# Half-height transposes in the scores' buffers and longer runs of one kind on TensorE, in an attention and mixture-of-experts kernel

## The chip, the cores and the metric

The kernel runs on one core of a Trainium2 chip. The metric is the device time of one execution in microseconds, the median of several runs. The engines are named as in the profile: PE (TensorE's matmuls), PEld (its weight loads), DVE (VectorE), ACT (ScalarE), POOL (GpSimd) and SP (SyncE, which here issues most DMAs).

## The reference

The input is 8 batches of 1024 tokens with 512 features in fp32. A layer norm and an attention with 16 heads of 32 features come first, then a second layer norm and a mixture of 8 experts. Queries, keys and values are not products with weights: they are cosines and sines of scaled features.

```python
theta_q = xh / (1.0 + jnp.abs(w_q)) + b_q + t * phi_q      # same for k
Q = concatenate([cos(theta_q), sin(theta_q)])              # 64 per head; same for K
V = cos_v + sin_v                                          # 32 per head
scores = einsum('bqhd,bkhd->bhqk', Q, K) / scale           # causal
out = einsum('bhqk,bkhd->bqhd', softmax(scores), V)
theta_out = out / (1.0 + jnp.abs(w_out)) + b_out
x = x + cos(theta_out) + sin(theta_out)
# then, on layernorm(x): each token goes to its top 2 of 8 experts, 160 places
# per expert and batch; expert = relu(buf @ W1 + b1) @ W2 + b2, gated, added to x
```

## The kernel before, in words

The attention is worked off in 32 steps `n`, one for each batch `b` and block `c` of 128 features (four heads), `b, c = divmod(n, 4)`. Each step has two head pairs. What follows are the names that matter.

- `scores(pair, h)` makes the transposed scores of one head pair for half `h` of the queries. `tiles_of(h)` gives its tiles: three for half 0, seven for half 1. The last tile of each half is 256 queries wide, the others 512 (one of them is made of 384 and 128). Each tile has two heads. Their keys and queries lie on rows 0 to 63 and 64 to 127, and they are multiplied by two matmuls that use 64 rows and 128 columns of the array each and write one PSUM bank each. The tile's two banks come from the pool `ps_sc`, which has two such tiles. ACT takes the exponential of both into `e`, and DVE zeroes the keys that lie ahead in the tiles on the diagonal (L590, the mask).
- `attend(n, pr, h, es)` multiplies those tiles by the values: two matmuls of 128 rows and 64 columns a tile, one for each head, into one bank of `ps_av`. At its end DVE scales the result into `av_sb`.
- `turn(pr, h, av_sb, p)` transposes `av_sb` by four full 128 x 128 transposes into a bank of the pool `ps_tr` (two banks), and DVE divides by the row sums, which stand among the columns, into `o_p`.
- `qk_pre(n)` transposes the normalized input of a step, again by fours into `ps_tr`, and DVE makes the angles of queries and keys from it (L463, then a shift in L395). `qk_abs`, `qk_sin` and `qk_post` turn them into cosines and sines on ACT and DVE. `v_pre` and `v_post` do the values, `o_pre` and `o_post` the output angle and the sum into `x_mid`, with the statistics of the second layer norm. A step's `qk_pre` runs two steps ahead, its `qk_abs`, `qk_sin` and values one step ahead, and `o_pre` and `o_post` one step behind.
- `router(b)` is a generator that picks the experts of a batch's tokens: `rows` (layer norm on DVE, and a DMA of each row tile to DRAM), `features` (four transposes into `ps_tr` and a copy into `xT`), `parts` (narrow matmuls of 32 columns), `whole` (their sum over the four groups), then the choice on DVE and a prefix sum on PE (`place`). It begins at the end of step `c = 0` of the next batch. Its rows and features fall in the first half of step `c = 1`, the last sums in that step's second half.
- `layernorm1` normalizes a later batch on DVE, in the first halves of steps `c = 0` and `c = 3` (in the first batch, of `c = 1` and `c = 2`).
- `experts` comes last and takes up the span from about 1470 us on. `gather` fetches the tokens of an expert by indirect DMA and transposes them; the first six of these gathers run inside the last attention step.

PE, DVE and ACT run in the order in which the program names their instructions: the kernel sets it by hand. The generators yield between their pieces. `run` takes two pieces of each of its generators in turn, and after each two, one piece of each generator in `aside` (such as the router, `v_pre`, `qk_abs`, `qk_pre`, a layer norm):

```python
e11, av10 = run(scores(pairs[1], 1), attend(n, 1, 0, e10), aside=asides)
```

So scores and products alternate on PE by about two tiles each, with transposes between them.

The exponentials are kept in eight buffers of 512 queries and two of 256 (`ep`), and a head half's product has one of two banks (`ps_av`). [...]

Of the kernel before, what the change touches and what calls it, by code (L numbers as in the profile page):

```python
# [71 lines left out]
def preln_attn_moe_kernel(  # L72
# [61 lines left out]
    avp = to_router.pool("avp", 2, **left)  # L134
# [52 lines left out]
    ps_tr = to_end.pool("ps_tr", 2, space=PSUM)  # L187
# [12 lines left out]
    ps = ps_tr.tile([P, 6 * NCH], F32, name="ps_t")  # L200
# [99 lines left out]
    ps_sc = to_pairs.pool("ps_sc", 2, space=PSUM)  # L300
# [27 lines left out]
    def load_b1():  # L328
        t = own.tile([E * NHC, P], F32, name="vec_in")
        nc.sync.dma_start(t, b1.rearrange("e (c p) -> (e c) p", p=P))  # L330
        ps = ps_tr.tile([P, P], F32, name="ps_t")
        nc.tensor.transpose(ps, t, ident)
        nc.vector.tensor_copy(b1_t, ps)
        two = b1_t.rearrange("p (e h q) -> p e h q", e=E, h=2)
        nc.vector.tensor_tensor(b1_more, two[:, :, 1, :], two[:, :, 0, :], ALU.subtract)
# [3 lines left out]
    def load_mid(b):  # L339

        xt = xmp.tile([P, NTT, D], F32, name="x_mid")
        for h in range(2):
            nc.sync.dma_start(
                xt[:, 4 * h : 4 * h + 4, :], token_tiles(x[b])[:, 4 * h : 4 * h + 4, :]
            )
        st = small.tile([P, NTT, NCH, nc.vector.BN_STATS_DIM], F32, name="st_mid")
        mid_tiles[b] = (xt, st)
# [100 lines left out]
    def qk_pre(n):  # L448

        b, c = divmod(n, NCH)  # L450
        base = bases.pop(n)
        p = qkt.tile([P, 2, S], I32, name="qk_f")
        r = qkt.tile([P, 2, S], I32, name="qk_r")
        for h in range(2):
            yield
            ps = ps_tr.tile([P, 4, P], F32, name="ps_t")
            for t in range(4):
                nc.tensor.transpose(  # L458
                    ps[:, t, :], xn_tiles[b][h][:, t, c * P : (c + 1) * P], ident
                )  # L460
            for i in range(2):
                cols = (slice(None), i, slice(512 * h, 512 * (h + 1)))
                nc.vector.scalar_tensor_tensor(  # L463
                    p[cols], ps.rearrange("p t q -> p (t q)"),
                    inv_qk[:, i * NCH + c : i * NCH + c + 1], base[cols], ALU.mult, ALU.add,
                )
        yield p, r
# [97 lines left out]
    def scores(pair, h):  # L565

        es = []
        for parts in tiles_of(h):
            n = sum(w for _, _, w, _ in parts)
            ps = ps_sc.tile([P, 2, 512], F32, name="ps_s")  # L570
# [21 lines left out]
            yield es  # L592

    def attend(n, pr, h, es):

        vt = v_tiles[n % 2]
        av = ps_av.tile([P, 512], F32, name="av")
        tiles = tiles_of(h)
        for i, parts in enumerate(tiles):
            if i:  # L600
                yield
            for kb, q0, w, at in parts:
                for a in range(2):
                    nc.tensor.matmul(  # L604
                        av[a * 64 : (a + 1) * 64, q0 - 512 * h :],
                        lhsT=vt[:, kb, 2 * pr + a, :], rhs=es[i][:, a, at : at + w],
                        start=kb == 0, stop=i + 1 == len(tiles),
                    )
        av_sb = avp.tile([P, 512], F32, name="av_sb")
        q = 2 * (n % NCH) + pr  # L610
        nc.vector.tensor_scalar(av_sb, av, inv_o[:, q : q + 1], None, ALU.mult)  # L611
        yield av_sb

    def run(*gens, aside=()):


        last, live = [None] * len(gens), list(range(len(gens)))
        while live:
            for i in list(live):
                for _ in range(2):  # L620
                    try:
                        got = next(gens[i])
                        last[i] = got if got is not None else last[i]
                    except StopIteration:
                        live.remove(i)
                        break
                for g in aside:
                    next(g, None)
        return last
# [7 lines left out]
    def turn(pr, h, av_sb, p):  # L637

        ps = ps_tr.tile([P, 4, P], F32, name="ps_t")
        for t in range(4):  # L640
            nc.tensor.transpose(ps[:, t, :], av_sb[:, t * P : (t + 1) * P], ident)  # L641
        av = ps.rearrange("p t (a f) -> p t a f", a=2)
        rec = small.tile([P, 4, 2, 1], F32, name="rec")
        nc.vector.reciprocal(rec, av[:, :, :, DH : DH + 1])
        dst = p.rearrange("p (t a d) -> p t a d", a=HPC, d=DH)
        nc.vector.tensor_tensor(
            dst[:, 4 * h : 4 * h + 4, 2 * pr : 2 * pr + 2, :], av[:, :, :, :DH],
            rec.to_broadcast([P, 4, 2, DH]), ALU.mult,
        )
# [12 lines left out]
    def router(b):  # L662
# [10 lines left out]
        prob = small.tile([P, NTT, E], F32, name="prob")  # L673
# [14 lines left out]
        def features(xn, xT, i):  # L688
            ps = ps_tr.tile([P, NCH, P], F32, name="ps_t")
            for c in range(NCH):  # L690
                nc.tensor.transpose(ps[:, c, :], xn[:, c * P : (c + 1) * P], ident)  # L691
            copy(xT[:, :, i * P : (i + 1) * P], ps)

        def parts(xT):

            ps = ps_tr.tile([P, 2 * P], F32, name="ps_t")
            for c in range(NCH):
                nc.tensor.matmul(  # L698
                    ps[32 * c : 32 * (c + 1), :], lhsT=wr_sb[:, c, :], rhs=xT[:, c, :],
                    start=True, stop=True, tile_position=(0, 32 * c),  # L700
                )
            lg = row2.tile([P, 2 * P], F32, name="lg", bufs=1)
            copy(lg, ps)
            return lg

        def whole(g, lg):

            ps = ps_tr.tile([P, 2, E], F32, name="ps_t")
# [10 lines left out]
        ahead = rows(0)  # L719
        yield "tiles"  # L720
        lg, xT_ = None, None
        for g in range(NTT // 2):
            if g:
                lg = parts(xT_)
            xT_ = row2.tile([P, NCH, 2 * P], F32, name="xT", bufs=1)
            for i in range(2):
                xn = ahead
                if 2 * g + i + 1 < NTT:
                    ahead = rows(2 * g + i + 1)
                features(xn, xT_, i)  # L730
                if i == 0:
                    yield
# [4 lines left out]
        lg = parts(xT_)  # L737
# [50 lines left out]
        place = ps_tr.tile([P, NTT, E], F32, name="ps_t")  # L788
# [119 lines left out]
    def gather(i):  # L908
# [3 lines left out]
        for j in range(2 * nh):  # L912
# [6 lines left out]
            ps = ps_tr.tile([P, NCH, P], F32, name="ps_t")  # L919
            for c in range(NCH):  # L920
                nc.tensor.transpose(ps[:, c, :], xg[:, c * P : (c + 1) * P], ident)  # L921
            nc.vector.tensor_copy(xe[:, :, j // nh, j % nh * P : (j % nh + 1) * P], ps)  # L922
# [153 lines left out]
    def experts(ending):  # L1076
        pools["hp"] = to_end.pool("hp", NHQ, **right)
        pools["ps_p"] = to_end.pool("ps_p", 6, space=PSUM)
# [63 lines left out]
    for n in range(NCK + 1):  # L1142
        live, more, late = n < NCK, n + 1 < NCK, last is not None
# [4 lines left out]
        if live:  # L1148
            pos_n = trig.tile([P, S], F32, name="o_p")
            (e00,) = run(scores(pairs[0], 0))  # L1150
        if n == 0:
            qk_st = rest(qk_pre(1))
            angle(*qk_st)
        if late:
            e11, av10, pos = last
            turn(1, 0, av10, pos)

        if not live:
            break

        if n == 1:
            load_mid(0)


        asides, places, v_box = [], [None], [None]
        if more:
            asides += [keep(places, qk_abs(qk_st)), keep(v_box, v_pre(n + 1))]
        if route is not None and c > 0:
            asides.append(part(route))
        if not more:  # L1170
            asides.append(first_rows)
# [4 lines left out]
        elif c == 3 and b + 2 < B:  # L1176
            asides.append(layernorm1(b + 2, 0))
        av11, e01 = run(
            attend(n - 1, 1, 1, e11) if late else iter(()), scores(pairs[0], 1),
            aside=asides,  # L1180
        )
        for g in asides:
            rest(g)
        if more:
# [12 lines left out]


        (av00,) = run(attend(n, 0, 0, e00))
        if late:  # L1200
            turn(1, 1, av11, pos)
            o_st = o_pre(n - 1, pos)
# [7 lines left out]
        (av01,) = run(attend(n, 0, 1, e01))  # L1210
        turn(0, 0, av00, pos_n)
# [4 lines left out]
        (e10,) = run(scores(pairs[1], 0))  # L1216
        turn(0, 1, av01, pos_n)
# [3 lines left out]

        places = [None]
        asides = [keep(places, qk_pre(n + 2))] if n + 2 < NCK else []
        if route is not None and c > 0:
            asides.append(part(route))
        e11, av10 = run(scores(pairs[1], 1), attend(n, 1, 0, e10), aside=asides)
        for g in asides:
            rest(g)
        if n + 2 < NCK:
            qk_st = places[0]  # L1230
# [6 lines left out]
        last = (e11, av10, pos_n)  # L1237
        pairs = next_pairs if more else None
    turn(1, 0, av10, pos_n)
    (av11,) = run(attend(NCK - 1, 1, 1, e11))  # L1240
    turn(1, 1, av11, pos_n)
# [53 lines left out]
```

## Time and profile before

| | |
|---|---|
| median of 3 runs | 3486.86 us (3486.4 to 3488.84) |
| the profiled execution, its own time | 3486.65 us |
| its span, first to last instruction | 3484.9 us |
| mean granted TensorE clock | 0.992 |
| busy in 100 to 1200 us (attention) | PE 1034.9, DVE 950.4, ACT 806.5, POOL 100.9 us |
| busy in 1500 to 3485 us (experts) | PE 1957.7, DVE 1231.3, ACT 272.1, POOL 228.7 us |
| PE's waits in 100 to 1420 us | for ACT's exponentials 32.6 us; for router rows 15.7, `xT` 12.0, `av_sb` 9.2, `lg` 7.5 us (DVE) |

A row of the costliest groups gives the line, engine and operation, the tile written and the tiles read, the shape, how often, the busy time in us and the mean of one in ns, and the idle time ahead of it with what ended most of it. For a matmul the shape begins with rows x columns of the array that it uses ("64*128"). Each fp32 matmul that is not a transpose appears as two passes, so two records. The ends of matmuls are modelled, so a busy PE may hide short gaps; the distance from one start to the next doesn't.

### The profile page before, as it was taken

The numbers are of one execution on the slowest core, as the hardware profiler recorded it, in microseconds if no ns is written. First come the engines' busy times: TensorE is split into PE (matmuls) and PEld (weight loads), VectorE is DVE, ScalarE is ACT, GpSimd is POOL, SyncE is SP. The second block draws the span as 40 slices with busy tenths as digits, with TensorE's granted clock in tenths as the row PEclk, the third lists the DMA queues.
The fourth block names the chain that finished last, engine by engine and source line by source line (L and its number), as shares of the span: only waits on it lengthen the run. The fifth ranks groups of instructions, "written<-read, shape, count | busy, mean of one in ns | idle before, by whom it ended". The sixth has DMA issues, their size and how long they took to land.

```text
span 3484.9 us, 43387 instructions
## 1 busy us (share of the span) xinstructions
PE 3302.9 (95%) x15974; PEld 2171.9 (62%) x15974; DVE 2469.3 (71%) x5569; ACT 1315.7 (38%) x1609; POOL 391.1 (11%) x346
## 2 busy tenths in 40 slices
PE   3899999999999999889999999999999999999998
PEld 1344444444444444458868868778778688688687
DVE  7897989898989878574684585576566747746844
ACT  5676767676767676420120111111111101101201
POOL 0000202020202020232101101100110111011010
PEclk9999999999999999999999999999999999999999
DMA  4434343434353434142232322422322323322321
GB/s 142 125 93 148 90 154 91 154 91 153 91 178 89 132 87 135 46 137 39 75 106 46 112 61 49 112 55 61 106 46 67 103 43 76 103 38 76 105 40 25
DMA packets 242684, 320.45 MB, mean 92 GB/s; under 512 B 30312, under 2 KB 163112, under 8 KB 230056
## 3 DMA queue, kind: packets, MB, share of 16 engines
q1 hardware_dynamic: 220304, 275.54, 26.7%
q0 software_dynamic: 22080, 42.10, 6.8%
q8 instruction: 127, 2.08, 0.2%
q14 instruction: 85, 0.70, 0.1%
q10 hardware_dynamic: 88, 0.02, 0.0%
HBM read 188.67 MB, written 61.82 MB: 72 GB/s over the span
## 4 chain that ended last, share of the span: by engine, by line
PE 79%; DVE 12%; ACT 5%; issue 2%; DMA 1%; POOL 0%; POOLq 0%; DVEq 0%; ACTq 0%; SPq 0%
PE ps_p L1010 27%; PE ps_p L965 24%; PE av L604 11%; PE ps_s L574 11%; ACT e L580 4%; PE ps_t L641 2%; DVE e L590 1%; PE ps_t L921 1%; PE ps_t L458 1%; PE ps_t L691 1%; DVE qk_c L405 1%; DVE av_sb L611 1%; DVE qk_r L405 1%; DVE xn L679 0%; PE ps_t L698 0%
## 5 line engine op out<-in xcount | busy, mean ns | idle before, releaser
L580 ACT ACTIVATE e<-ps_s 128x1024 f32<-128x1024 f32 (+1 forms) x640 | 564.5, 937 | 389.8 <-PE ps_s L574 385.9
L574 PE MATMUL ps_s<-qk 64*128 64x512 f32 (+3 forms) x3072 | 607.7, 512 | 62.0 <-ACT e L580 40.4
L1010 PE MATMUL ps_p<-w,hid 128*128 128x256 f32 x2560 | 569.4, 380 | 0.0
L604 PE MATMUL av<-e,v 128*64 128x512 f32 (+3 forms) x3072 | 557.4, 499 | 5.8 <-DVE e L590 5.8
L1010 PEld LDWEIGHTS ps_p<-w,hid 128*128 128x128 f32 x2560 | 484.5, 190 | 66.3
L574 PEld LDWEIGHTS ps_s<-qk 64*128 64x128 f32 x3072 | 277.9, 187 | 326.1 <-issue 160.2
L1010 PE MATMUL ps_p<-w_t,hid 128*128 128x256 f32 x1920 | 430.5, 379 | 1.3 <-DVE w_t L886 1.3
L604 PEld LDWEIGHTS av<-e,v 128*64 128x64 f32 x3072 | 195.5, 138 | 322.1 <-issue 264.2
L1010 PEld LDWEIGHTS ps_p<-w_t,hid 128*128 128x128 f32 x1920 | 361.7, 190 | 49.7 <-DVE w_t L886 2.1
L965 PE MATMUL ps_p<-xe_s,t 128*128 128x256 f32 (+1 forms) x1024 | 299.8, 436 | 3.4 <-DVE t L950 3.4
L965 PE MATMUL ps_p<-xe,w 128*128 128x256 f32 (+1 forms) x1024 | 298.3, 434 | 0.2
L965 PE MATMUL ps_p<-xe,t 128*128 128x256 f32 (+1 forms) x1024 | 296.8, 433 | 0.0
L657 POOL DMA_INDIRECT slot_d<-token,slot x128 | 149.4, 1167 | 1146.9 <-issue 636.9
L590 DVE TENSOR_TENSOR e<-e,seen 128x256 f32<-128x256 f32 (+1 forms) x384 | 184.4, 510 | 118.3 <-ACT e L580 115.1
L965 PEld LDWEIGHTS ps_p<-xe_s,t 128*128 128x128 f32 x1024 | 194.6, 191 | 87.3 <-DVE t L950 7.9
L1039 ACT COPY p<-ps_p 128x256 f32<-128x256 f32 x40 | 14.7, 368 | 612.5 <-PE ps_p L1010 612.5
L965 PEld LDWEIGHTS ps_p<-xe,t 128*128 128x128 f32 x1024 | 194.4, 190 | 80.5
L965 PEld LDWEIGHTS ps_p<-xe,w 128*128 128x128 f32 x1024 | 192.8, 190 | 82.5 <-DVE hid L983 5.9
L1032 POOL DMA_INDIRECT out_dram<-y,slots x80 | 126.4, 1580 | 671.5 <-DVE y L1027 528.6
L914 POOL DMA_INDIRECT xg<-xn_d,source x80 | 78.3, 979 | 1026.8 <-PE ps_t L921 1017.1
L922 DVE COPY xe<-ps_t 128x512 f32<-128x512 f32 x80 | 55.3, 691 | 194.9 <-PE ps_t L921 194.3
L980 ACT ACTIVATE p<-ps_p,b_t 128x256 f32<-128x256 f32 (+1 forms) x128 | 65.5, 512 | 330.5 <-DVE y L1026 170.0
(193 smaller groups left out, 3874.0 us busy)
## 6 DMA issues: line engine op xcount, KB each, us to landing
w<-in_L_ffn_W_dram SPq DMA_DIRECT2D x256, 256.0 KB, 3.2
qk<-qk_c SPq DMA_DIRECT2D x128, 256.0 KB, 4.5
qk<-qk_r SPq DMA_DIRECT2D x128, 256.0 KB, 4.6
w<-in_L_ffn_W_dram SPq DMA_DIRECT2D x64, 512.0 KB, 7.1
qk_base<-base_d SPq DMA_DIRECT2D x29, 1024.0 KB, 5.1
xn_d<-xn SPq DMA_DIRECT2D x72, 256.0 KB, 2.0
x_mid<-in_L_attn_x_dram SPq DMA_DIRECT2D x16, 1024.0 KB, 8.5
out_dram<-x_mid SPq DMA_DIRECT2D x8, 2048.0 KB, 11.7
```

The source lines that it names most:

```text
L405: nc.vector.scalar_tensor_tensor(out, f.bitcast(F32), LIFT, s, ALU.add, ALU.mult)
L574: nc.tensor.matmul(ps[:, a, at : at + w], lhsT=pair[r, 1, kb * P : (kb + 1) * P], rhs=pair[r, 0, q0 : q0 + w], start=True, stop=True,)
L580: nc.scalar.activation(e, ps[:, :, :n], AF.Exp, scale=UNIT * UNIT / math.sqrt(2 * DH))
L590: nc.vector.tensor_tensor(own_keys, own_keys, k, ALU.mult)
L604: nc.tensor.matmul(av[a * 64 : (a + 1) * 64, q0 - 512 * h :], lhsT=vt[:, kb, 2 * pr + a, :], rhs=es[i][:, a, at : at + w], start=kb == 0, ...
L641: nc.tensor.transpose(ps[:, t, :], av_sb[:, t * P : (t + 1) * P], ident)
L657: nc.gpsimd.indirect_dma_start(out=slot_d[b], out_offset=bass.IndirectOffsetOnAxis(ap=idx, axis=0), in_=src, in_offset=None,)
L914: nc.gpsimd.indirect_dma_start(out=xg, out_offset=None, in_=xn2_d[i % 2], in_offset=bass.IndirectOffsetOnAxis(ap=source[:, e, j0 + j, None ...
L965: nc.tensor.matmul(ps, lhsT=weights[:, k, :], rhs=rows[:, k, :], start=k == 0, stop=k == 1)
L980: nc.scalar.activation(p1, product(b11, a11), AF.Identity, bias=b1_t[:, e * NHC + q : e * NHC + q + 1])
L1010: nc.tensor.matmul(ps, lhsT=hs[k][:, part, cols], rhs=ws[k][weight], start=k == 0, stop=k == NHQ - 1,)
L1032: nc.gpsimd.indirect_dma_start(out=out, out_offset=bass.IndirectOffsetOnAxis(ap=meta[:, e, jj[r], 0:1], axis=0), in_=ys[r], in_offset=None ...
```

## The change

The transposes of the attention stage are cut in halves of 64 rows: the upper 64 rows of a block go to one bank and the lower 64 to the other, by two transposes that use 64 rows and 128 columns of the array, as a score matmul does. Their target is a tile of `ps_sc`, which now has three tiles; `ps_tr` is opened only for the experts. The router's sums take tiles of `ps_sc` too. `turn` takes both query halves of a head pair at once, and `qk_pre` both token halves. The order is written out in longer runs: three product tiles, five score tiles, three products, four scores, three products, one score, a `turn`, the eight remaining products, five scores, a `turn`, three products, five scores, and then `qk_pre` in one piece at the step's end. Asides now go on by one piece after each score tile. `rows` are made two at a time. The pools `avp` and `once` change to fit (three `av_sb`, single buffers for `st_mid` and `prob`).

```diff
-    ps_tr = to_end.pool("ps_tr", 2, space=PSUM)
+    ps_sc = to_pairs.pool("ps_sc", 3, space=PSUM)
+    def two_banks():
+        return ps_sc.tile([P, 2, 512], F32, name="ps_s")
+    def by_halves(turned, src):
+        for a in range(2):
+            r = slice(a * 64, (a + 1) * 64)
+            nc.tensor.transpose(turned[:, a, :], src[r, :], ident[r, r])
...
 def qk_pre(n):
-        for h in range(2):
-            yield
-            ps = ps_tr.tile([P, 4, P], F32, name="ps_t")
-            for t in range(4):
-                nc.tensor.transpose(
-                    ps[:, t, :], xn_tiles[b][h][:, t, c * P : (c + 1) * P], ident
...
+        ps = two_banks()
+        for t in range(NTT):
+            by_halves(
+                ps[:, :, t * 64 : (t + 1) * 64],
+                xn_tiles[b][t // 4][:, t % 4, c * P : (c + 1) * P],
+            )
...
-    def turn(pr, h, av_sb, p):
-        ps = ps_tr.tile([P, 4, P], F32, name="ps_t")
-        for t in range(4):
-            nc.tensor.transpose(ps[:, t, :], av_sb[:, t * P : (t + 1) * P], ident)
+    def turn(pr, halves, p):
+        ps = two_banks()
+        for t in range(NTT):
+            by_halves(
+                ps[:, :, t * 64 : (t + 1) * 64],
+                halves[t // 4][:, t % 4 * P : (t % 4 + 1) * P],
+            )
...
+        products = [attend(n, 0, h, es[h], halves[0]) for h in range(2)]
+        if late:
+            products.insert(0, attend(n - 1, 1, 1, e11, halves1))
+        ahead = [scores(pairs[0], h, es[h]) for h in range(2)]
...
+        def with_asides(count):
+            for _ in range(count):
+                some(1, *ahead)
+                for g in asides:
+                    next(g, None)
+        if late:
+            some(3, *products)
...
+            with_asides(5)
+        some(2, absolutes)
+        if late:
+            some(3, *products)
+        with_asides(4)
+        some(2, absolutes)
+        some(3, *products)
+        with_asides(1)
...
+        if late:
+            turn(1, halves1, pos)
+            o_st = o_pre(n - 1, pos)
...
+        some(NTT + 2, *products)
...
+        with_asides(5)
+        turn(0, halves[0], pos_n)
...
+        some(3, attend(n, 1, 0, es[0], halves1))
+        with_asides(5)
+        if n + 2 < NCK:
+            qk_st = rest(qk_pre(n + 2))
```

Here `some(k, *gens)` takes the next `k` pieces of the generators, one generator after the other. The router's `features` handles two row tiles in one piece:

```diff
-        ahead = rows(0)
+        ahead = [rows(0), rows(1)]
         yield "tiles"
...
+                ps = two_banks()
+                for i, xn in enumerate(xns):
+                    for c in range(NCH):
+                        at = (NCH * i + c) * 64
+                        by_halves(ps[:, :, at : at + 64], xn[:, c * P : (c + 1) * P])
+                for a in range(2):
+                    copy(
...
+            if g + 1 < NTT // 2:
+                ahead = [rows(2 * g + 2), rows(2 * g + 3)]
             if g:
                 whole(g - 1, lg)
             yield
```

The last batch's router and all gathers but the first expert's keep full transposes.

## The prediction

> **What bounds the kernel now.** I read the page's busy shares first, then its costliest groups, then the busy times by stretch, then the timelines of three engines inside one step.
>
> ```profile
> PE 3302.9 (95%) x15974; PEld 2171.9 (62%) x15974; DVE 2469.3 (71%) x5569; ACT 1315.7 (38%) x1609; POOL 391.1 (11%) x346
> ...
> L574 PE MATMUL ps_s<-qk 64*128 64x512 f32 (+3 forms) x3072 | 607.7, 512 | 62.0 <-ACT e L580 40.4
> ```
>
> TensorE is busy 95% of the span, but the experts (from 1470 us on) are not touched; only the attention stage before them counts. There one batch is four steps. I cut it at the four starts of the wide sine of L482 (the third is batch 3's second; columns: span of the stretch, then busy us of PE, PEld, DVE, ACT, POOL):
>
> ```profile
> 555.17:594.78 39.60, 38.53 (x218) 17.15 (x218) 35.80 (x76) 31.81 (x32) 14.30 (x12) 1.00 0.32 80
> 594.78:645.10 50.32, 45.30 (x280) 21.91 (x278) 42.59 (x95) 31.92 (x32) 0.20 (x2) 1.00 0.53 154
> 645.10:687.87 42.76, 39.97 (x233) 17.92 (x230) 33.86 (x75) 31.95 (x33) 0.00 (x0) 1.00 0.53 165
> 687.87:728.70 40.84, 39.75 (x226) 18.15 (x228) 37.46 (x86) 31.81 (x32) 5.01 (x4) 1.00 0.30 79
> ```
>
> I call them A, B, C, D: 173.5 us a batch. PE is the fullest, but DVE is at 80 to 92% and ACT at 63 to 80%, both in program order: whoever speeds up PE soon waits for them. Now the inside of PE's busy time (start, us, then the group):
>
> ```profile
> 604.45 1.99 PE L574 MATMUL ps_s<-qk 64*128 64x512 f32 x8
> 606.37 1.94 PE L604 MATMUL av<-e,v 128*64 128x512 f32 x12
> 608.25 0.66 PE L458 MATMUL ps_t<-ident,xn 128*128 128x128 f32 x4
> 608.83 1.99 PE L574 MATMUL ps_s<-qk 64*128 64x512 f32 x8
> 610.75 0.66 PE L458 MATMUL ps_t<-ident,xn 128*128 128x128 f32 x4
> 611.34 0.65 PE L604 MATMUL av<-e,v 128*64 128x256 f32 x4
> ```
>
> Three shapes of the array alternate: 64*128 (scores), 128*64 (products), 128*128 (transposes).
>
> [...] inside a run, pairs of 512-column passes start 0.429 us apart, so eight score records (four pairs) are 1.72 us of work, but the next group starts 1.92 us later (604.45 to 606.37): 0.20 us a run of scores. Products: the run at 606.37 is also 1.72 us of work and takes 1.87, 0.156 a run. Four transposes start 0.109 apart, 0.44 us, and take 0.585, 0.148 a run. [...] two 64-row, 128-column score passes, each with its own load, start every 0.109 us. [...]
>
> **The change, part by part.**
> *Fewer mode changes.* In the order of instructions up to the experts' first product, runs of one mode go from 254 scores, 252 products, 260 full-array and 28 narrow router runs to 223, 159, 37 and 28: half transposes use the scores' mode and stand next to scores. Cost before 254 x 0.20 + 252 x 0.156 + 260 x 0.148 + 28 x 0.14 = 132.5 us; after 223 x 0.20 + 159 x 0.156 + 37 x 0.148 + 3.9 = 78.8. **Minus 53.7 us**, all on PE's path.
> *Half transposes.* Two per former one. A pair loads 128 columns in each row group and streams 64. Not shown before: at best 0.055 us a pair (half the columns), at worst 0.218 (no overlap). I take 0.109, the pair of score passes: no change.
> *VectorE.* Same elements: two reciprocals (0.198) and two fixed parts fewer a step, under 0.6 us; the 512-element operations of L463 and L692 stay four and two in number at 0.74 and 0.68. The strided 64-blocks I take at the same price (range 0 to +10%, 0.5 us a step). DMA queues and POOL keep their instructions. The router's rows now store in twos (256 KB each, 2.0 us to landing on the page); with two buffers the next two wait for both stores, which land 2 us before DVE gets there. SP's loads of qk are issued 10 us and more ahead of use, and `load_mid(0)`, issued later by half a step, is used a step later.
> *ScalarE.* The same instructions; their distance decides what PE waits for. From the timeline of ACT:
>
> ```profile
> 592.33 1.14 ACT L399 ACTIVATE v_p<-v_p,split_c 128x1024 f32<-128x1024 uint16 x1
> 593.49 1.28 ACT L482 ACT_TABLE_LOAD   x1
> 594.78 2.00 ACT L482 ACTIVATE qk_c<-qk_c,quarter_c 128x2048 f32<-128x2048 f32 x1
> 596.69 1.89 ACT L402 ACTIVATE qk_r<-qk_r 128x2048 f32<-128x2048 int32 x1
> 598.49 1.99 ACT L402 ACTIVATE t_r<-t_r 128x1024 f32<-128x1024 int32 x2
> 600.49 1.28 ACT L580 ACT_TABLE_LOAD   x1
> 602.16 2.43 ACT L580 ACTIVATE e<-ps_s 128x1024 f32<-128x1024 f32 x3 [0.38 <-PE ps_s L574]
> ```
>
> From 592.33 to 602.16 no exponential runs: 9.8 us. I laid one new step out by hand: PE at 0.86 us a wide score tile (0.43 a narrow one) plus the run costs; exponentials every 0.92 us (0.50), the first 0.27 after its scores' last pass is issued, its buffer free 1.08 after its start. Zero is the first run of products.
> - P3 to 2.7; five score tiles to 6.8, unhindered: the third buffer removes the stall of 0.56 that three tiles have before. P3 to 9.6, four tiles to 13.2, P3, one tile, turn at 16.0 to 16.9, eight products to 23.1.
> - ACT runs without a pause from 10.8: four exponentials, two squares, the narrow exponential, square, table, sines, table, and starts the next exponential at 26.9. PE has three free buffers for the next run, filled at 25.4; the fourth tile waits until 27.9: **2.5 us**. Before, this stretch loses 0.56 + 1.66.
> - The rest is PE's: the next step begins at 38.1. Work 33.2, ten runs 1.8, waits 2.8 and seams.
>
> So a plain step is 38.1. VectorE in the same step: `qk_pre`, now one block at the step's end, is through L463 and L395 4.6 us after PE has gone on; it is in time for the next step's masks (4.9). Then the kinds of stretches:
> - A: 38.1, and in six of seven batches 1.3 of lateness that D's layernorm leaves. 39.3 (39.6 before).
> - D: `places` takes a buffer among five score tiles and its readers follow `v_post` on DVE: +1.3. 39.4 (40.8).
> - C: `parts` and `whole` do the same at the end of the router: +1.9, exp of `prob` +0.3. 40.3 (42.8).
> - B: the router's tiles. DVE's chain ahead of them:
>
> ```profile
> 611.21 2.70 DVE L463 SCALAR_TENSOR_TENSOR qk_f<-ps_t,inv_qk,qk_base 128x512 int32<-128x512 f32 x4
> ...
> 616.07 1.22 DVE L395 TENSOR_SCALAR qk_r<-qk_f 128x2048 int32<-128x2048 int32 x1
> 617.21 1.11 DVE L669 BATCH_NORM_AGGREGATE mv<-st_mid 128x2 f32<-128x24 f32 x8
> ...
> 621.25 0.55 DVE L679 TENSOR_SCALAR xn<-x_mid,mv,rstd 128x512 f32<-128x512 f32 x1
> ```
>
> The aggregates, the roots and the first row of tokens (5.2 us from 616.07's end) now follow that late block: 4.6 + 1.1 + 2.9 + 0.5 = 9.1 us into the step, when PE has been at the first `features` since 3.7: 5.4 us of wait, against 1.2 at 621.85 before. What follows in the ring of three (score, `parts`, `features`, score, `whole`) costs PE 1.0 at the first `parts` (its xT copies stand behind a mask and `v_pre`), 1.6 at the second `features` (rows behind a mask and a bias addition), 0.8 at the fifth score tile, then little. Work of features, parts and sums 5.1, their mode changes 2.1. Step c = 1 reaches its sine 16.0 later than a plain one: **54.1 (50.3)**.
>
> Sum: A to D 173.1 against 173.5 a batch, seven times: -3. The first batch has no router; its stretches of 42.9 and 39.8 fall to about 39.0 and 38.3: -5. The start and the last step (six gathers, whose PE waits of 5.15, 3.32 and 1.27 us depend on landings) I take as unchanged, plus or minus 5. Experts: same instructions, 0. Together -8 of the profiled execution's 3486.65 (span 3484.9; the median, 3486.86, lies within 0.3): **3478**. So of 53.7 us saved on modes, about 45 come back as waits.
>
> **Rivals.** A measurement here tells 0.2%, 7 us, from nothing.
> 1. *Slower: VectorE's round trip in every lap of the router.* Transposes and router sums now draw on the scores' three buffers, so a late DVE copy stops scores too. If laps three and four each wait 2.6 us as the first pair does (1.0 + 1.6), with none of them caught up, B gains 5.2 more, times seven, 36: 3514. It decides once DVE is still over 2 us behind PE at the third `parts`. For it: 42.6 us busy in B. Against: P3 between laps two and three gives DVE 2.7 us.
> 2. *Faster: the mode changes come through whole.* If ACT's trigonometry is covered (a shorter backlog at the narrow tile) and the router waits no longer than now, all 53.7 stay: 3433. For it: half of the runs of products end. Against: 9.8 us without exponentials against 9.3 us of work and buffers.
> 3. *Halves do not overlap.* 1016 pairs at +0.109 are 111 us; the third of them ahead of the eight products hides in ACT's wait: +78, 3556. Against: the 0.109 of score passes. At 0.055 a pair it turns into some -28 instead.
> That the order doesn't change is excluded: the counts of runs come from it.
>
> **How the numbers follow.** Forecast 0.42 (3455 to 3497), rival 1 0.28, rival 2 0.22, rival 3 0.08. Half of the forecast's mass lies below 3480, a quarter within 7 us of 3487. Faster 0.22 + 0.22, and a little of rival 3's other end: 0.45; same 0.13; slower 0.42. The range 3430 to 3535 leaves out the lower half of rival 2's spread and rival 3. The likeliest case alone: 3455 to 3497.
>
> **What would show it.** Runs of products in a plain step take work + 0.156 five times, not eight; half transposes 0.87 us per eight tiles; fourth score tile of the second head pair waits about 2.5 us for L592's exponential; the first `features` of a batch waits about 5 us for a row of L684; stretches of some 38 to 40, 54, 40, 39. It is wrong if B is under 51, if A is under 37 or over 41, or if half transposes start over 0.12 apart.

## The result, and the profile after

The changed kernel takes 3544.16 us (median of four runs, 3540.82 to 3551.25) against 3486.76: ratio 1.0166, interval 1.0148 to 1.0184, some 57 us slower. The forecast was 3478. The profiled execution took 3551.25 us with a span of 3549.5 and a mean granted clock of 0.957; before it had 3486.65, 3484.9 and 0.992.

The page of the kernel after, first the busy shares, then the granted clock by fortieths of the span, then the group of the scores:

```profile
PE 3276.8 (92%) x16986; PEld 2175.1 (61%) x16986; DVE 2462.8 (69%) x5439; ACT 1308.0 (37%) x1609; POOL 389.7 (11%) x346
...
PEclk9899989898989898899999999999999999999999
...
L586 PE MATMUL ps_s<-qk 64*128 64x512 f32 (+3 forms) x3072 | 615.2, 535 | 47.5 <-ACT e L592 23.3
```

PE is busy 26 us less than before although it has more instructions, and it waits more: 92% of a longer span. Its clock row, a row of 9s before, has an 8 in many slices of the attention, and the same 3072 score passes take 535 ns each instead of 512. The four stretches of batch 3 (columns as in the prediction; the last three are granted clock, DMA share, GB/s):

```profile
568.09:609.44 41.35, 38.01 (x248) 17.56 (x248) 36.87 (x74) 31.33 (x33) 12.46 (x13) 0.91 0.32 77
609.44:671.34 61.90, 53.02 (x362) 24.88 (x360) 44.45 (x92) 31.99 (x33) 0.00 (x0) 0.82 0.50 154
671.34:714.01 42.67, 39.12 (x256) 18.62 (x254) 33.61 (x72) 31.80 (x34) 0.00 (x0) 0.92 0.43 124
714.01:752.14 38.13, 33.05 (x224) 15.42 (x220) 34.30 (x78) 31.44 (x33) 4.68 (x4) 0.99 0.33 84
```

All four had a clock of 1.00 before. Only D keeps it, and D is the one that became clearly shorter (40.8 to 38.1). Means over seven batches (six for D), in us:

| stretch | before | forecast | after | after minus forecast | times | in all |
|---|---|---|---|---|---|---|
| A | 39.6 | 39.3 | 40.6 | +1.3 | 7 | +9 |
| B | 50.7 | 54.1 | 60.2 | +6.1 | 7 | +43 |
| C | 43.1 | 40.3 | 42.6 | +2.3 | 7 | +16 |
| D | 40.8 | 39.4 | 38.1 | -1.3 | 6 | -8 |

With the first batch (forecast -5, measured +6.7 with the start) and the end from the last wide sine on (forecast 0, measured +4.1) this makes the 73 us between forecast and profiled execution, but for 3 us by which the forecast's one batch lay below the mean.

What PE waited for, over the whole span (in all, times, longest):

```profile
PE ps_s L200 <- DVE xn L684: 64.3, 15, 6.0
PE ps_s L200 <- DVE av_sb L622: 52.7, 17, 8.9
PE ps_s L737 <- DVE lg L730: 24.8, 7, 3.5
```

In batch 3 these are waits of 2.6 to 6 us: 3.8 at the seam of D and A, 2.6 at the seam of A and B, 6.0 and 2.9 in B, 3.5 in C. The timeline of PE in B shows what follows one (start, us, the group, the idle time before it):

```profile
606.01 0.41 PE L200 MATMUL ps_s<-ident,av_sb 64*128 64x64 f32 x8
609.00 0.69 PE L200 MATMUL ps_s<-ident,av_sb 64*128 64x64 f32 x8 [2.58 <-DVE av_sb L622]
609.62 8.98 PE L614 MATMUL av<-e,v 128*64 128x256 f32 x36
618.53 4.32 PE L586 MATMUL ps_s<-qk 64*128 64x512 f32 x24
...
629.72 0.71 PE L200 MATMUL ps_s<-ident,xn 64*128 64x64 f32 x16
630.36 2.80 PE L614 MATMUL av<-e,v 128*64 128x512 f32 x12
633.09 1.13 PE L586 MATMUL ps_s<-qk 64*128 64x512 f32 x4
640.18 1.12 PE L200 MATMUL ps_s<-ident,xn 64*128 64x64 f32 x16 [5.97 <-DVE xn L684]
643.90 1.08 PE L725 MATMUL ps_s<-xT,wr_sb 128*32 128x256 f32 x8
647.89 1.22 PE L200 MATMUL ps_s<-ident,xn 64*128 64x64 f32 x16 [2.91 <-DVE xn L684]
```

The eight products after the turn take 8.98 us where the same 36 records take 6.2 in a stretch at full clock (shown below). The 16 half transposes take 0.71 ahead of the wait for the rows and 1.12 after it. The record of the clock says why: the granted share is 0.5 from 608.36 to 615.18 and from 639.08 to 656.14, and 1.00 between them. The wait from 606.4 to 609.0, at the seam of A and B, cost 2.6 us by itself and then 2.7 in the eight products.

I counted such half-clock spells in the clock record from 100 us to the experts' first product, and PE's busy time in them. Before: 4 spells, 20.5 us long, PE busy for 19.7 of them. After: 36 spells, 252.6 us, **PE busy for 197.3 us of them**. In them a pair of 512-column product passes starts 0.853 us after the last, outside them 0.429 (medians). So at full clock that work would take about half as long, and the spells cost PE some 99 us by this estimate. (The expectation of e1 says 34 spells and 86 us: it counts up to 1470 us and with another estimate of the work.)

The record also shows when the clock falls. Its 84 changes between the first and the last lie on one grid of 3.413 us, to within 2 ns. Of the grid's intervals between 100 and 1440 us, PE entered 322 at full clock. In 33 of them it was busy for 47% of the interval or less, and half clock followed every one. In the other 289 it was busy for 48% or more, and half clock followed none. In other runs the border is less sharp: in the kernel before the clock falls after intervals of up to 56% and stays after some from 41% on, in e6 it falls after up to 62% and stays after some from 48% on; the ends of matmuls are modelled. So in the changed kernel the place of a wait in the grid counted too: it sets how much of each interval is left (see D's wait of 1.84 us, below).

### The profile page after: what moved, and what is told of

Read it like the earlier page. It is cut to its first block, busy times and chain, and to the rows that moved or that the text cites. A ratio compares the mean times of both kernels' runs of the same rounds, so it can differ in the third digit from the quotient of the medians.

```text
span 3549.5 us, 45378 instructions
## 1 busy us (share of the span) xinstructions
PE 3276.8 (92%) x16986; PEld 2175.1 (61%) x16986; DVE 2462.8 (69%) x5439; ACT 1308.0 (37%) x1609; POOL 389.7 (11%) x346
## 4 chain that ended last, share of the span: by engine, by line
PE 68%; DVE 16%; ACT 9%; DMA 4%; issue 3%; POOL 0%; SPq 0%; DVEq 0%; POOLq 0%; ACTq 0%
PE ps_p L1043 26%; PE ps_p L998 24%; PE av L614 7%; PE ps_s L586 7%; ACT e L592 4%; DVE qk_f L476 2%; DVE e L602 2%; DMA xn_d<-xn 1%; PE ps_s L200 1%; DMA slot_d<-token,slot 1%; DVE st L367 1%; DVE qk_r L407 1%; PE ps_t L954 1%; ACT qk_c L495 1%; ACT qk_f L411 1%
## 5 line engine op out<-in xcount | busy, mean ns | idle before, releaser
L586 PE MATMUL ps_s<-qk 64*128 64x512 f32 (+3 forms) x3072 | 615.2, 535 | 47.5 <-ACT e L592 23.3
L614 PE MATMUL av<-e,v 128*64 128x512 f32 (+3 forms) x3072 | 565.8, 516 | 6.7 <-DVE e L602 6.7
L614 PEld LDWEIGHTS av<-e,v 128*64 128x64 f32 x3072 | 211.5, 144 | 318.4 <-issue 278.0
L1017 ACT ACTIVATE hid<-hid 128x256 f32<-128x256 f32 (+1 forms) x128 | 60.1, 470 | 317.4 <-DVE hid L1016 317.4
```

The lines of the kernel that those rows point to most:

```text
L586: nc.tensor.matmul(ps[:, a, at : at + w], lhsT=pair[r, 1, kb * P : (kb + 1) * P], rhs=pair[r, 0, q0 : q0 + w], start=True, stop=True,)
L614: nc.tensor.matmul(av[a * 64 : (a + 1) * 64, q0 - 512 * h :], lhsT=vt[:, kb, 2 * pr + a, :], rhs=es[i][:, a, at : at + w], start=kb == 0, ...
L1017: nc.scalar.activation(h11, h11, AF.Relu)
```

## The experiments

The theory: **the waits halve PE's clock**, and that is what the forecast lacks. The rivals: the waits themselves are too long because rows come late (rival 1's round trip), or because DVE's layer norm of a later batch delays `av_sb`; and the half transposes cost more than they save. Times of before in the same sessions were 3488 us.

**e1_warm: keep PE busy in its longest waits.** Nothing is moved. PE gets more to do: pairs of spare matmuls into the tile that the transposes or sums then overwrite.

```diff
+    def keep_warm(ps, count):
+        for _ in range(count):
+            for a in range(2):
+                r = slice(a * 64, (a + 1) * 64)
+                nc.tensor.matmul(
+                    ps[:, a, :], lhsT=ident[r, :], rhs=inv_v[r, :], start=True, stop=True
+                )
...
+                keep_warm(ps, (5, 2, 0, 0)[g])        # features
+                keep_warm(ps, 3 if g == 3 else 0)     # whole
-            turn(1, halves1, pos)
+            turn(1, halves1, pos, 3 if c in (0, 3) else 0)
```

> Spare score-shaped matmuls (64 rows, 128 columns of the array, 512 wide) are put into the tile that the next transposes or sums overwrite: five pairs ahead of the first features of a batch, two ahead of the second, three ahead of the last whole, three ahead of turn(1) in the steps with a layer norm. No result uses them. Theory 1, the slow clock: the waits for VectorE are about those of my sum, and the rest of the loss (some 66 us over the forecast) is PE running at half clock after each of them, 86 us of work done in 34 slow spells; with PE kept busy the clock stays up and the time falls by 40 to 60 us, to about 3495, B to some 55, A to 39. Theory 2, the waits alone: the spells lie in stretches where PE would have waited for VectorE anyhow; then the time moves by less than 10 us, about 3540.

Measured: 3500.13 us, ratio 1.0033 (1.0021 to 1.0046): **44 us less than the changed kernel, with more work on PE**. Its stretches A and B (batch 3):

```profile
557.05:595.72 38.67, 38.02 (x262) 17.92 (x264) 36.31 (x74) 31.32 (x32) 14.36 (x11) 1.00 0.32 83
595.72:651.14 55.42, 50.85 (x384) 23.84 (x384) 43.90 (x92) 31.99 (x33) 2.90 (x2) 1.00 0.56 172
```

The clock is 1.00 again. Over all batches A to D are 38.5, 55.9, 41.5, 38.9: close to the forecast's 39.3, 54.1, 40.3, 39.4. PE's timeline at the place shown above:

```profile
592.29 2.74 PE L206 MATMUL ps_s<-inv_v,ident 64*128 64x512 f32 x12
594.87 0.78 PE L200 MATMUL ps_s<-ident,av_sb 64*128 64x64 f32 x16
595.58 6.24 PE L622 MATMUL av<-e,v 128*64 128x256 f32 x36
```

The spare matmuls fill the wait for `av_sb`, and the 36 product records behind it take 6.24 us instead of 8.98. Half-clock spells fall from 36 to 14, PE's busy time in them from 197.3 to 58.0 us. Half of the difference is 70 us, of which 44 show in the time. The theory holds. What remains in B, 55.9, is time at nearly full clock (0.91 to 1.00 in its seven batches).

**e2_router_late: start the router's tiles five score tiles later in step c = 1**, then two pieces at a time, so that the rows are made before PE asks.

```diff
-        if route is not None and c > 0:
+        if route is not None and c == 1:
+            asides += [later(10, part(route))] * 2
+        elif route is not None and c > 0:
             asides.append(part(route))
```

(`later(k, gen)` yields `k` times before it goes on to `gen`. It stands in the list twice, so ten yields are five score tiles.)

> In step c = 1 the router's pieces begin five score tiles later, at the sixth, and go on two at a time, so that VectorE has caught up with its block at the step boundary when PE reaches the first features. Both theories: the wait of about 6 us for the first rows goes, and with it most of the half-clock spell. B falls from about 60 to 51 to 53, the whole by 50 to 65 us, to about 3485. If instead the rival of the round trip in every lap rules (scores stopped by late copies through the shared three tiles), B stays above 57 and the gain is under 20 us.

Measured: 3511.23, ratio 1.0072 (1.0055 to 1.0088), 33 us less than the changed kernel. B fell to 53.8, not to the 51 to 53 expected, and the saving is below the 50 to 65 expected. The row waits went, and a new one came, in PE's timeline:

```profile
634.73 0.64 PE L725 MATMUL ps_s<-xT,wr_sb 128*32 128x256 f32 x8 [3.46 <-DVE xT L710]
```

The first `parts` now waits 3.5 us for its `xT` copy, and 29 spells remained, with PE busy for 170.8 us in them. Removing one wait did not restore the clock here, with another of 3.5 us in its place and those of A and C untouched.

**e3_norm_moved and e4_late_and_moved: move the later batch's layer norm out of the first halves of steps c = 0 and c = 3** into the second halves of c = 1 and c = 3, to free DVE ahead of `av_sb` and rows; e4 has e2's edit too. In the first batch the layer norm of step 0 is left out, since step 2 makes it again.

```diff
-        elif c == 0 and b + 1 < B:
-            asides.append(layernorm1(b + 1, 1))
-        elif c == 3 and b + 2 < B:
-            asides.append(layernorm1(b + 2, 0))
...
+        if b > 0 and c == 1 and b + 1 < B:
+            asides.append(layernorm1(b + 1, 1))
+        elif c == 3 and b + 2 < B:
+            asides.append(layernorm1(b + 2, 0))
```

> layernorm1 of a later batch goes from the first halves of steps c = 0 and c = 3 to the second halves of c = 1 and c = 3. Theory: the waits of turn(1) for av_sb (52.7 us in all) come from the layer norm that stands ahead of av_sb in VectorE's queue, and each is followed by a slow spell over the eight products. A falls from 41.4 to about 38.5; C rises by up to 2 since its sums wait longer behind the norm; the whole falls by 5 to 30 us, to about 3525. Rival: VectorE is the bound there anyway, and the wait only moves to another place: within 10 us of 3544.

> The edits of e2 and e3 together. If VectorE's order is the cause and the mode savings of 54 us are real, the time falls below that of before: B about 51, A about 38.5, C about 42, D 38, 170 a batch against 173.5, so about 3460 to 3475. If the savings in mode changes were not real or are bound up with the waits, it stays at 3487 or above.

Both expectations failed. e3 took 3575.09, ratio 1.0244 (1.0227 to 1.0261), 31 us slower than the changed kernel; e4 3536.36, ratio 1.0135 (1.0118 to 1.0151), 25 slower than e2 alone. PE's waits in e3:

```profile
PE ps_s L586 <- ACT e L592: 52.0, 31, 3.1
PE ps_s L586 <- DVE qk_f L476: 19.2, 13, 2.8
PE ps_s L200 <- DVE av_sb L622: 17.0, 11, 8.9
```

The wait that it was made for did shrink, from 52.7 to 17.0 us. But ACT's exponentials now hold PE up for 52.0 us (23.3 in the changed kernel), and `qk_f` for 19.2 (2.9); there are 42 half-clock spells. The second halves end with `qk_pre`. That the layer norm delayed DVE there, and that the exponentials came late because their masks and angles did, is argued, not traced further.

**e5_full_height: the order of the changed kernel with full transposes**, in `turn` and `qk_pre`.

```diff
-            by_halves(
-                ps[:, :, t * 64 : (t + 1) * 64],
-                halves[t // 4][:, t % 4 * P : (t % 4 + 1) * P],
-            )
+            nc.tensor.transpose(
+                ps[:, t // 4, t % 4 * P : (t % 4 + 1) * P],
+                halves[t // 4][:, t % 4 * P : (t % 4 + 1) * P], ident,
+            )
```

> The changed kernel with full 128 x 128 transposes again in turn and qk_pre, into the same two-bank tiles and in the new order; the router keeps its halves. Theory: the half height is worth its price in the sum: each of 96 groups of eight transposes would take 0.87 us plus one more change of mode (0.15) instead of 0.49, about 0.53 us, 51 us in all, of which the 32 groups ahead of the eight products may hide in ACT's wait: 3575 to 3595. Rival: what is saved on PE comes back as waiting wherever it is, because VectorE sets the pace: within 10 us of 3544.

Measured: 3563.91, ratio 1.0214 (1.0197 to 1.0231), 20 us slower than the changed kernel. A `turn` in its timeline of PE:

```profile
589.52 1.09 PE L643 MATMUL ps_s<-ident,av_sb 128*128 128x128 f32 x8
```

Eight full transposes take 1.09 us, the 16 halves 0.71: the halves are cheaper, and so no cause of the loss. The difference is below the 31 to 51 us expected and above the rival's 10; that part of these groups lies ahead of a wait for ACT or DVE would explain it, but is not shown.

**e6_late_warm: e2's later start, and e1's filling** in the waits that then remain (three pairs at the turn in c = 0 and 3, four at the first `parts` of a batch, three at the last `whole`).

> The router begins late as in e2, and spare matmuls stand ahead of the turn in the steps with a layer norm (three pairs), ahead of the first parts of a batch (four) and ahead of its last whole (three). Slow-clock theory: e2's gain of 33 and e1's of 44 are for different places in part (e1's of A and C remain to be had), so about 3475 to 3490, B to 51, C to 41, A to 39. Rival, the waits alone: no better than e2, 3505 to 3515.

Measured: 3475.09, ratio 0.9959 (0.9945 to 0.9973), 69 us below the changed kernel and below the one before. Stretches 38.4, 51.8, 41.0, 39.2; 13 spells, with PE busy for 65.6 us in them. As expected.

**e7_sums_late: e6 with the router's last sums five score tiles later**, unfilled, to take away the `lg` wait rather than fill it.

```diff
-            asides.append(part(route))
+            asides.append(later(5, part(route)))
```

> As e6, and the router's last sums and its places come five score tiles later in the second halves of steps 1 and 2 (behind turn(0), where VectorE no longer has the trigonometric products and v_post in front of them); no spare matmuls at the last whole. C loses its wait of 3.5 us for lg and falls to about 39.5, the rest as e6: 3460 to 3480, which would be below the kernel before (3487). If VectorE is the pace-setter everywhere, C stays over 41 and the time with e6's.

Measured: 3484.9, ratio 0.999 (0.9981 to 0.9999): 10 us worse than e6, and C at 41.5 instead of 39.5, so the expectation failed. Its waits of PE:

```profile
PE ps_s L594 <- ACT e L600: 33.6, 17, 2.2
PE ps_s L756 <- DVE lg L744: 17.5, 16, 2.0
```

The longest `lg` wait shrank from the 3.5 us of the changed kernel to 2.0, and the half-clock spells stay few without filling there (15, in e6 13). But the sums now stand among the last score tiles of the step; the waits for `lg` in all rose from 7.3 in e6 to 17.5, and those for ACT from 18.6 to 33.6.

**e8_full_height_warm: e6 with e5's full transposes.** With the clock restored, this prices the halves in a kernel with few half-clock spells.

> e6 with the full 128 x 128 transposes in turn and qk_pre, the edit of e5: the price of the half height where the clock is kept up. Theory: in e5 slow spells and VectorE's waits blurred it (20 us of the 51 worked out); here PE sets the pace in more places, so 25 to 45 us over e6's 3475, about 3500 to 3520, D up by about 1.5 to 2.2. Rival, VectorE and ScalarE set the pace: again 20 us or less.

Measured: 3493.41 (15 runs, 3486 to 3506), ratio 1.0017 (1.0009 to 1.0025), 18 us above e6. The rival's figure, 20 us or less, held. In the profiled executions, which are 27 us apart, A, B, C and D are 1.1, 1.5, 0.9 and 0.8 us longer. So the halves of `turn` and `qk_pre`, with the changes of mode that full transposes bring back, are worth about 0.5% of the time in both pairs of kernels, with many half-clock spells (e5) and with few (e8).

**e9_first_batch: e6 without the layer norm that step 0 makes ahead of time.** In the first batch the second half of batch 1 is normalized in step 0 and again in step 2 (in the kernel before as well). The edit leaves out the first, as e3 did; filling at the turn is added in steps 1 and 2.

```diff
-        elif c == 0 and b + 1 < B:
+        elif c == 0 and 0 < b < B - 1:
             asides.append(layernorm1(b + 1, 1))
...
-            turn(1, halves1, pos, 3 if c in (0, 3) else 0)
+            turn(1, halves1, pos, 3 if c in (0, 3) or n < 3 else 0)
```

> e6 without the layer norm of step 0, which is made again in step 2, and with spare matmuls ahead of turn(1) in steps 1 and 2 too. The 8.9 us in which that turn waits for av_sb in step 1 come from VectorE's backlog of the first steps: 4 to 12 us under e6, about 3465. If the backlog has another cause (the angles of the first block), no change from 3475.

Measured: **3463.23 (3461.32 to 3464.18), ratio 0.9926 (0.9913 to 0.9939)**, the fastest of all, 81 us below the changed kernel and 25 below the one before. Its A and B of batch 3:

```profile
547.30:586.08 38.78, 38.01 (x262) 17.86 (x264) 36.44 (x74) 31.31 (x32) 15.09 (x10) 1.00 0.32 82
586.08:637.71 51.63, 49.24 (x372) 23.36 (x372) 43.83 (x92) 31.76 (x33) 3.77 (x3) 0.97 0.60 185
```

The mean stretches are 38.5, 51.3, 41.0 and 39.2; A is where it was in e1 and B 8.9 below the changed kernel's, 0.7 above the one before. But the wait for `av_sb` that the edit was made for is still there. PE's waits at that turn, in e3 (no layer norm in step 0, no filling) and in e9 (2.7 us of spare matmuls ahead of it):

```profile
128.74 0.69 PE L200 MATMUL ps_s<-ident,av_sb 64*128 64x64 f32 x8 [8.91 <-DVE av_sb L622]
129.32 0.69 PE L200 MATMUL ps_s<-ident,av_sb 64*128 64x64 f32 x8 [6.33 <-DVE av_sb L630]
```

So the layer norm of step 0 does not cause it: DVE works without a pause ahead of this `av_sb`, on the base of the next angles and on the layer norm of step 1 itself among others; which of them counts was not tested. The first four steps take 171.0 us, in e6 175.3. The layer norm left out shortens the first of the four by about 2 us, in e3 as in e9; the fourth is 3 us shorter than in e6, where the filling in step 2 lets 36 product records take 6.24 us instead of 8.90 (single profiles). Of the other 8 us below e6, about 5 lie behind the last wide sine and 3 in B, neither of which the edit touches; they stay open (e6's own runs spread from 3468.6 to 3479.7).

All kernels with their half-clock spells from 100 us to the experts' first product:

| kernel | us | half-clock spells | their length, us | PE busy in them, us |
|---|---|---|---|---|
| before | 3486.76 | 4 | 20.5 | 19.7 |
| after | 3544.16 | 36 | 252.6 | 197.3 |
| e1 | 3500.13 | 14 | 71.7 | 58.0 |
| e2 | 3511.23 | 29 | 194.6 | 170.8 |
| e3 | 3575.09 | 42 | 249.2 | 198.0 |
| e4 | 3536.36 | 36 | 208.2 | 188.2 |
| e5 | 3563.91 | 36 | 218.5 | 177.3 |
| e6 | 3475.09 | 13 | 78.5 | 65.6 |
| e7 | 3484.9 | 15 | 81.9 | 70.7 |
| e8 | 3493.41 | 12 | 78.5 | 65.2 |
| e9 | 3463.23 | 10 | 47.8 | 39.8 |

## Why the prediction was wrong, step by step

**The failed step: the sum takes PE's speed as constant.** Every term of work was at the durations of a kernel whose attention ran at full clock, and the change was to open waits of 5.4, 2.5 and 1.6 us by the prediction's own account. The sum has no term for what PE does after them. The clock record of the changed kernel has it: spells at a granted 0.5, of 3.4, 6.8, 10.2, 17.1 and 20.5 us, multiples of 3.41 on one grid; those up to 1440 us began after intervals in which PE was busy for 47% or less. In the wait of 2.6 us at the seam of A and B, the clock fell when PE had stood for 1.9 us. e1 puts the price at 44 us, of the 66 that the median missed the forecast by.

D shows a wait that brings a spell in some places and none in others. There PE waits 1.84 us for ACT in every batch. In the changed kernel the grid cuts all six of these waits so that PE is busy for 52% or more of both intervals, and no spell follows; in e6 and e9, one of 3.4 us follows in four of six, and D takes 39.7 to 39.8 instead of 38.1. Where the grid cuts the wait there is not shown. The same place in the changed kernel and in e6:

```profile
722.10 0.70 PE L586 MATMUL ps_s<-qk 64*128 64x256 f32 x4 [1.84 <-ACT e L592]
723.01 1.99 PE L586 MATMUL ps_s<-qk 64*128 64x512 f32 x8 [0.21 <-ACT e L592]
...
350.18 0.70 PE L594 MATMUL ps_s<-qk 64*128 64x256 f32 x4 [1.85 <-ACT e L600]
351.10 3.60 PE L594 MATMUL ps_s<-qk 64*128 64x512 f32 x8 [0.21 <-ACT e L600]
```

**The waits.** Those of the router were foreseen in place and cause; the others only in part:
- The first `features` waits 5.97 us for a row of L684 (forecast 5.4).
- The wait of 2.5 for ACT at the fourth score tile was laid out for every plain step. In D it comes at the third, where `places` has a buffer too: 1.84 us, and 0.21 at the next (lines above). In A and B it does not come, nor does it in e1's A and B at full clock. There PE waits for `av_sb` just before, which may be what lets ACT catch up.
- The second `features` waits 2.91 (1.6). The prediction let the row stores land 2 us before DVE gets there. They do not: DVE's timeline has the row itself held up.

```profile
639.49 1.00 DVE L684 TENSOR_SCALAR xn<-x_mid,mv,rstd 128x512 f32<-128x512 f32 x2
647.20 1.17 DVE L684 TENSOR_SCALAR xn<-x_mid,mv,rstd 128x512 f32<-128x512 f32 x2 [1.16 <-DMA xn_d<-xn]
```

  This 1.16 is nearly the size of the miss. More row buffers might take it away; that was not tried.
- Missed: the turns at the two seams of A wait 3.8 and 2.6 us for `av_sb`, behind the layer norm on DVE (e3, which moves it, cuts these waits from 52.7 to 17.0 in all). The prediction had 1.3 us of lateness there. It also had 1.9 for `parts` and `whole` in C together, where `whole` alone waits 3.5 for `lg`.

In these waits the engines took nothing that the program names behind. PE stood 5.97 us for the first rows and took the score tile behind them at 641.06, after the 16 transposes of 640.18. ACT was in its table loads and sines from 712.71 to 721.02 while the score tile begun at 717.47 stood. DVE stood 1.16 us ahead of the row at 647.20, and copied the `lg` that PE had ended at 644.98 behind it, at 649.22.

Of B's 6.1, e1 returns 4.3. The other 1.8 is the size of the longer waits at the two `features` (0.6 and 1.3), but the missing wait for ACT and the shorter transposes work the other way in B, so this split is not shown. A and C: e1 gives back 2.1 of A's and 1.1 of C's; C's other 1.2 goes with the longer wait for `lg`.

**The mode changes** (from one shape of the array to another) were right. In the changed kernel, at full clock, the record behind a 512-column score pass starts 0.423 us after it if its shape is the same (a half transpose or a narrower score pass), and 0.519 if it is a product (medians). A run of 16 product records is 2.575 us of work and takes 2.73, a run of 20 score records 3.44 and takes 3.64: 0.155 and 0.20 as before. So the price of a run did not change and, by the count of runs, the 53.7 us were saved on PE. No run measures them by themselves: with full transposes e8 is level with the kernel before (1.0017), so what e6 and e9 gain can't be put down to the modes alone. D takes 38.1, the figure laid out by hand for a plain step, but that is luck. The forecast for D was 39.4, and D is made of other terms: 2.05 of waits for ACT, and 3.0 of the wait for `av_sb` that begins in D (in batch 3 from 749.1 to D's end at 752.14).

**The half transposes** were mis-sized: at full clock a pair starts 0.062 us after the last (the median in the changed kernel), near the lower bound of 0.055 and not at 0.109, which a full transpose of the same block takes. A group of 16 halves takes 0.64 us to the next run (629.72 to 630.36). In the half-clock spells a pair takes 0.107. By the prediction's count, 1016 pairs at 0.047 less are 48 us of PE's time. In the whole time, e5 and e8 show 20 and 18 us for three quarters of the pairs and the changes of mode together. The error was in the kernel's favour: it hid a part of the loss.

**The first batch** was to give 5 us and cost 6.7. PE waits 8.9 us there for `av_sb`; the prediction carried the gain of a plain step into a batch whose own waits it had not laid out. The layer norm of step 0 is not their cause (e3 and e9 above). **The end**, +4.1, lies inside the 5 allowed.

**Rivals.** Rival 1 had the sign, slower, by 27, but not the mechanism: laps three and four were not to catch up because DVE would be behind. In the trace they run without a wait (the third `parts` starts at 661.37, at full clock), and it is DVE that waits for PE, 2.88 us at 654.96; the half clock (639.08 to 656.14) lies on the first two laps. Filling the waits, which leaves DVE's work as it is, takes 4.3 us out of B. Rival 2's size, 3433, was not reached by any kernel here, e9 at 3463 being the nearest. Rival 3 is excluded by the 0.062; its aside, some -28 at 0.055 a pair, has the right sign. Of the forecast's own signs of being wrong, B under 51 and A under 37 or over 41, the second did not show in the mean A of 40.6 but does in five of the seven batches (41.4 to 41.8). For B there was no upper bound, and the loss came there. One reading in the prediction is off without effect: the 5.2 us of aggregates and roots run from the start at 616.07, not from its end; the sum uses their parts, 1.1, 2.9 and 0.5.

**What stays open.** Which of the remaining spells are due to which wait; what holds up `av_sb` in step 1 for 8.9 us; why B is still 1.8 over the forecast when the waits are filled; why e3 raises the waits for exponentials as much as it does; and 8 of the 12 us between e6 and e9.

## What to carry to other kernels

An edit that shortens PE's work but opens waits of 1.8 to 6 us on it can pay twice, since in these runs half-clock spells of 3.4 to 20.5 us went with many of them: price the spell with the wait. Look at the granted clock by stretch, not only at busy shares, and if a wait can't be removed, give PE spare matmuls into a tile that it is about to overwrite, as e1 and e6 do. Before a wait is removed by moving work on another engine, ask what stands at the new place: e3 and e7 exchanged one wait for others. And look whether the wait that an edit was made for is gone: e9 became faster and kept it.

## What the runs showed of the hardware that was not expected

- Added work made the kernel faster: 8 to 20 spare records on PE at a time, and 44 us less in all (e1).
- The clock changes on a fixed grid of 3.413 us. In the changed kernel it fell after every interval in which PE was busy for 47% or less, and after no other; a wait of 1.84 us was followed by a spell in four of six batches of e6 and in none of the changed kernel's. A spell of 17.1 us stands over a wait of 6.0 with one of 2.9 within it.
- Two half transposes of 64 rows and 128 columns, each with its own load, start 0.062 us after the pair before them (0.107 at half clock); a full transpose of the same block takes 0.109 (groups of eight blocks: 0.71 against 1.09 us).
